# A fixed order of weights and additions on VectorE in the gather passes of a graph network

## Chip, core and metric

The kernel runs on one core of one Trainium2 chip. The metric is device time in microseconds (us) of one execution; less is better. PE is TensorE's matmuls and PEld its weight loads, DVE is VectorE, ACT is ScalarE, POOL is GpSimd, SP is SyncE. "L720" is line 720 of the kernel before the change.

## What is computed

Two layers, each a graph convolution followed by a feed-forward part, work on 6250 nodes with 256 float32 features and 100000 edges that are sorted by target node. The change touches the two sums over edges in the graph convolution of the second layer, which the code calls layer 1. Cut to what matters, the reference does this:

```python
def _hconv(x, src, dst, ew, w1, b1, w2, b2, g, b):
    h = relu(x @ w1 + b1)
    msg = ew[:, None] * h[src]                             # one row for each edge
    agg = segment_sum(msg, dst, num_segments=x.shape[0])   # sum by target node
    h = agg @ w2 + b2
    return relu(_bn(h, g, b))

residual = x
h = _hconv(x, src, dst, ew, c1_w1, ...)      # first pass
h = relu(_bn(h, bn1_g, bn1_b))
h = _hconv(h, src, dst, ew, c2_w1, ...)      # second pass
h = _bn(h, bn2_g, bn2_b)
out = relu(h + residual)
```

## The kernel before

Nodes are handled in 49 tiles of 128. The node values `h` of a convolution are in SBUF (`X`) and also in a table in DRAM. The sums by target node are in SBUF (`sums`, a view of the buffer `wide`, which is the name that the profile shows), as 49 blocks of 128 nodes.

The edges are cut into work items of 128 edges that all end in one block of targets. There are 830 items. Since the edges are sorted and the low targets are frequent, the first 407 items belong to the first 13 blocks. These 13 blocks are not gathered edge by edge: their edge weights have been written earlier into a dense matrix in DRAM (`S`), and a block's sum is a product of that matrix with the node tiles. The other 423 items are gathered. Both happen beside each other, in one loop, `gather_pass`, which runs once for each convolution: the first pass and the second pass.

For each gathered item k the loop issues:

- the **gather** (L720): POOL starts an indirect DMA that fetches the 128 source rows of `h` from the table into a buffer `g`. There are ten such buffers, so gather k can start when product k-10 is done.
- the **weights** (L591, in `chosen`): DVE writes a 128x128 matrix `sw` that has each edge's weight in the column of its target. Ten buffers.
- the **product** (L725): PE multiplies `sw` with `g` into a PSUM buffer `pm`. There are six, so product k can start when addition k-6 is done. In float32 a product shows as two weight loads and two matmuls in the profile.
- the **addition** (L727): DVE adds `pm` to the block of `sums` that the item belongs to. The block's number is read from a table on the chip: every 32 items one read loads 32 of these numbers for DVE (`block_of`).

Between the items the generator `dense_parts` puts the dense products: 13 blocks times 49 node tiles are 637 products (L1280) of a tile of `S` with a tile of `X`, accumulated over 49 into one of two PSUM buffers `dps`; after 49 DVE adds the block to `sums` (L1282). The tiles of `S` come by DMA through SP (L1274), seven tiles in a load of 448 KB, into the buffer `wide_b`, which holds two blocks. The loop asks for dense products so that they keep in proportion to the items:

```python
while done * (NK - k0) < (k - k0) * DB * NT:
    done += 1
    next(beside, None)
```

The text of the loop does not settle the order on an engine. A scheduler reorders the recorded instructions when the program is built, within their dependencies and the buffers; each engine then runs its own list strictly in order and waits by semaphores for the others. Only where the code says `keep_in_program_order` do instructions keep the place that the text gives them. In the passes of the kernel before nothing says so.

If the edges do not fit the dense form, another branch gathers all 830 items. It is in the program but is not taken here.

Of the kernel before, what the change touches and what calls it, by code (L numbers as in the profile page):

```python
# [7 lines left out]
F32 = mybir.dt.float32  # L8
I32 = mybir.dt.int32
AF = mybir.ActivationFunctionType  # L10
OP = mybir.AluOpType
# [3 lines left out]
P = 128  # L15
# [18 lines left out]
KG = (NK + P - 1) // P  # L34
NB = NT - 1
EG = 8
X0 = 8
H0 = 1024
X1 = 4
# [24 lines left out]
SQ = ST // P  # L64
NST = (2 * N + X0 * (ST - 1)) // ST
RW = D + X0
BNC = 250
# [9 lines left out]
    ("L1_gnn_bn2_g", 2), ("L1_gnn_bn2_b", 2),  # L77
    ("L0_ffn_ln_g", 2 * X0), ("L0_ffn_ln_b", 2 * X0), ("L0_ffn_b1", 8 * X0),
    ("L1_ffn_sb1", 2), ("L1_ffn_sb2", 1), ("L1_ffn_eb1", X1),
# [12 lines left out]
def gnn_ffn_kernel(ctx: ExitStack, tc: tile.TileContext, a: dict, out: bass.AP):  # L92
    nc = tc.nc
# [79 lines left out]
    lane = const.tile([P, P], F32, name="lane")  # L173
# [13 lines left out]
    def weight(pool, name, shape, src, **kw):  # L187
        t = pool.tile(shape, F32, name=name, **kw)
        nc.sync.dma_start(t, src)
        return t  # L190
# [188 lines left out]
    dl = const.tile([P, KG * P], F32, name="dl")  # L379
    w_e = const.tile([P, KG * P], F32, name="w_e")  # L380
# [198 lines left out]
    def block_of(k, engine, k0=0):  # L579

        if k % 32 == 0 or k == k0:
            g, j = k // P, k % P // 32 * 32
            blocks[:] = nc.values_load_multi_w_load_instructions(
                bk_i[g:g + 1, j:j + 32], engines=[engine], min_val=0, max_val=NT - 1,
                skip_runtime_bounds_check_because="counts at most as many blocks")[1]
        return blocks[k % 32]

    def chosen(k, wp):

        sw = wp.tile([P, P], F32, name="sw")  # L590
        nc.vector.tensor_scalar(sw, lane, dl[:, k:k + 1], w_e[:, k:k + 1], op0=OP.is_equal, op1=OP.mult)  # L591
        return sw

    def product_of_cells(nodes, lp, tp, pp):

# [50 lines left out]
    def scatter_items(k0, k1, nodes, pools, step):  # L646

        ep, wp, ptp, pmp = pools

        def equals(k0, k1):  # L650

            n = k1 - k0
            eq = ep.tile([P, EG, P], F32, name="eq")
            ct = ep.tile([P, EG], F32, name="ct")
            for q0 in range(0, n, 4):
                q1 = min(q0 + 4, n)
                pt = ptp.tile([P, 4, P], F32, name="pt")
                for i in range(q0, q1):
                    nc.tensor.transpose(pt[:, i - q0, :], s_f[:, k0 + i:k0 + i + 1].to_broadcast([P, P]), ident)
                for i in range(q0, q1):  # L660
                    nc.vector.scalar_tensor_tensor(eq[:, i, :], pt[:, i - q0, :], s_f[:, k0 + i:k0 + i + 1],
                                                   upto2[:, P:], op0=OP.is_equal, op1=OP.mult,
                                                   accum_out=ct[:, i:i + 1])
            off = ep.tile([P, EG], F32, name="off")
            idx = ep.tile([P, EG], I32, name="idx")
            sf = s_f[:, k0:k1]
            nc.vector.tensor_scalar(ct[:, :n], ct[:, :n], 1.5, None, op0=OP.is_gt)
            nc.vector.tensor_scalar(off[:, :n], sf, spare, -1.0, op0=OP.subtract, op1=OP.mult)
            nc.vector.tensor_tensor(off[:, :n], off[:, :n], ct[:, :n], OP.mult)
            nc.vector.tensor_tensor(idx[:, :n], off[:, :n], sf, OP.add)  # L670
            return eq, idx

        groups = {}
        pcs = pmp.tile([P, 4, P], F32, name="pcs", bufs=1)

        def group(k):
            g0 = k0 + (k - k0) // EG * EG
            if g0 < k1 and g0 not in groups:
                groups[g0] = equals(g0, min(g0 + EG, k1))
            return groups.get(g0), k - g0  # L680

        def begin(k):
            (eq, _), i = group(k)
            sw = chosen(k, wp)
            pc = pcs[:, k % 4, :]
            nc.tensor.matmul(pc, sw, eq[:, i, :], start=True, stop=True)  # L686
            cT = wp.tile([P, P], F32, name="cT")
            nc.scalar.copy(cT, pc)
            return cT

        begun = [begin(k) for k in range(k0, min(k0 + 2, k1))]
        for k in range(k0, k1):
            step(k)
            cT = begun.pop(0)
            if (k - k0) % EG == 2:
                group(k + EG)
            if k + 2 < k1:
                begun.append(begin(k + 2))
            bv = block_of(k, mybir.EngineType.PE, k0)
            pm = pmp.tile([P, D], F32, name="pm")  # L700
            nc.tensor.matmul(pm, cT, nodes[:, bass.ds(bv, 1), :].rearrange("p o d -> p (o d)"), start=True, stop=True)  # L701
            m = wp.tile([P, D], F32, name="m", bufs=10)
            nc.scalar.copy(m, pm)
            (_, idx), i = group(k)
            nc.gpsimd.indirect_dma_start(  # L705
                out=accs[k % NACC], out_offset=bass.IndirectOffsetOnAxis(ap=idx[:, i:i + 1], axis=0),
                in_=m, in_offset=None, compute_op=OP.add)

    def gather_pass(table, sums, k0=0, parts=None):

        with tc.tile_pool(name="gg", bufs=10) as gp, tc.tile_pool(name="gw", bufs=10) as wp, \
                tc.tile_pool(name="gpm", bufs=6, space=PSUM) as pmp:
            beside = parts(pmp) if parts else iter(())
            done = 0
            for k in range(k0, NK):
                while done * (NK - k0) < (k - k0) * DB * NT:
                    done += 1
                    next(beside, None)
                g = gp.tile([P, D], F32, name="g")
                nc.gpsimd.indirect_dma_start(  # L720
                    out=g, out_offset=None, in_=table,
                    in_offset=bass.IndirectOffsetOnAxis(ap=s_i[:, k:k + 1], axis=0))
                sw = chosen(k, wp)
                pm = pmp.tile([P, 1, D], F32, name="pm")
                nc.tensor.matmul(pm[:, 0, :], sw, g, start=True, stop=True)  # L725
                at = sums[:, bass.ds(block_of(k, mybir.EngineType.DVE, k0), 1), :]
                nc.vector.tensor_tensor(at, at, pm, OP.add)  # L727
            for _ in beside:
                pass

# [213 lines left out]
    with tc.tile_pool(name="f0c", bufs=1) as fc:  # L944
        wr = weight(fc, "wr", [P, KD, X0], a["L0_ffn_Wr"].rearrange("(k p) e -> p k e", p=P))
        brs = fc.tile([P, X0], F32, name="brs")
        nc.sync.dma_start(brs, bass.AP(tensor=a["L0_ffn_br"].tensor, offset=a["L0_ffn_br"].offset, ap=[[0, P], [1, X0]]))
        NPAR = 2 * KD + H0 // P
# [3 lines left out]
        with tc.tile_pool(name="f0x", bufs=2) as xp, tc.tile_pool(name="f0s", bufs=1) as sp, \  # L952
# [149 lines left out]
            for t0 in range(0, NT, TG):  # L1102
                for j in range(2):
# [3 lines left out]
                    for t in range(t0, t0 + TG):  # L1107
                        at_q = xp.tile([P, NQ], F32, name="at_q", bufs=4)
                        nc.vector.tensor_scalar(at_q, lane[:, :NQ], high_f[:, j, t:t + 1], tok_f[:, t:t + 1],
                                                op0=OP.is_equal, op1=OP.mult)  # L1110
# [110 lines left out]
    with ExitStack() as gs:  # L1221
# [21 lines left out]
        sums = nodes  # L1243
# [19 lines left out]
        def graph_pass(table):  # L1263
            with tc.If(fit > 0) as cmp:
                gather_pass(table, sums, KF, dense_parts)
            with cmp.Else():
                gather_pass(table, sums)
# [236 lines left out]
```

## Time and profile before

| | |
|---|---|
| median of 3 runs | 4724.84 us (4722.76 to 4731.99) |
| profiled execution, its own time | 4707.7 us |
| its span, first to last instruction | 4705.9 us |
| mean granted clock of TensorE | 0.886 of full speed |
| busy share of the span | PE 79%, PEld 59%, DVE 41%, ACT 22%, POOL 47% |
| first pass | from 2851 to 3469 us of the span |
| second pass | from 3610 to 4237 us of the span |
| gathers L720 | 846, 952 ns each, 805.5 us busy |
| products L725 | 1692 matmuls, 536.3 us busy |
| dense products L1280 | 2548 matmuls, 726.7 us busy |
| weights L591 | 1269 (423 of them in an earlier stage), 359 ns each |
| additions L727 | 846, 416 ns each, idle 622.1 us before them |

How to read it: the profile is of one execution, whose time lies a little below the median. A group's row gives, behind the number of its instructions, their busy time in us, the mean of one in ns, and how long the engine stood idle just before them, with what ended most of that idle time ("<-PE dps L1280 382.0": 382.0 us ended by a dense product on PE). "issue" means that nothing the profile shows was waited for. The ends of matmuls are modelled. Idle time of an engine that does not set the pace costs nothing.

### The profile page before, as it was taken

How to read it: one execution, taken by the hardware profiler on the slowest of the kernel's cores; microseconds unless marked ns; L12 is line 12 of the kernel's file. 1: busy time of each engine (PE TensorE's matmuls, PEld its weight loads, DVE VectorE, ACT ScalarE, POOL GpSimd, SP SyncE). 2: the span in 40 equal slices, each digit the busy share in tenths (PEclk: the TensorE clock that was granted, in tenths of full speed). 3: DMA queues.
4: the chain of work that ended last, by engine and by line, in shares of the span. 5: the costliest groups of instructions: out<-in, count | busy, mean ns of one | idle time of the engine just before them, and what ended most of it. 6: DMA issues, size and time to landing. Idle time of an engine off the chain costs nothing. (4 is left out here: it accounts for less than half of the span.)

```text
span 4705.9 us, 52220 instructions
## 1 busy us (share of the span) xinstructions
PE 3695.4 (79%) x16041; PEld 2767.7 (59%) x16041; DVE 1920.3 (41%) x7365; ACT 1035.2 (22%) x2388; POOL 2207.9 (47%) x1914
## 2 busy tenths in 40 slices
PE   2046658787778577799999977888896888887999
PEld 1013436676667336688888866666655666663444
DVE  6134333333444467522212244444444444445443
ACT  2000103333334233122222231000014000006443
POOL 2766664877778400133333315666632666660000
PEclk8578778989999785799999989999997999988999
DMA  9432363766666743366666655555414555550000
GB/s 349 102 111 72 93 243 83 104 103 102 105 102 85 143 131 105 119 195 190 193 196 196 188 139 191 160 153 161 146 44 155 155 154 160 157 152 21 18 19 19
DMA packets 393990, 625.11 MB, mean 133 GB/s; under 512 B 58935, under 2 KB 293450, under 8 KB 393690
## 3 DMA queue, kind: packets, MB, share of 16 engines
q1 hardware_dynamic: 241860, 394.88, 25.7%
q0 software_dynamic: 144176, 197.85, 22.4%
q10 hardware_dynamic: 7654, 28.78, 1.7%
q8 instruction: 140, 2.29, 0.2%
q14 instruction: 160, 1.31, 0.1%
HBM read 456.84 MB, written 165.69 MB: 132 GB/s over the span
## 5 line engine op out<-in xcount | busy, mean ns | idle before, releaser
L720 POOL DMA_INDIRECT g<-table,s_i x846 | 805.5, 952 | 589.1 <-issue 174.3
L705 POOL DMA_INDIRECT acc<-m,idx x423 | 654.5, 1547 | 204.6 <-issue 74.4
L1280 PE MATMUL dps<-X,wide_b 128*128 128x256 f32 (+1 forms) x2548 | 726.7, 401 | 11.7 <-issue 11.6
L725 PE MATMUL pm<-g,sw 128*128 128x256 f32 x1692 | 536.3, 407 | 212.3 <-issue 125.3
L727 DVE TENSOR_TENSOR wide<-wide,pm 128x256 f32 x846 | 351.9, 416 | 622.1 <-PE dps L1280 382.0
L1280 PEld LDWEIGHTS dps<-X,wide_b 128*128 128x128 f32 (+1 forms) x2548 | 516.6, 203 | 97.6 <-issue 17.3
L563 POOL DMA_INDIRECT S<-hv,hc x395 | 427.5, 1082 | 275.7 <-issue 106.8
L725 PEld LDWEIGHTS pm<-g,sw 128*128 128x128 f32 x1692 | 320.0, 199 | 328.7 <-issue 209.3
L591 DVE TENSOR_SCALAR sw<-lane,dl,w_e 128x128 f32<-128x128 f32 x1269 | 440.3, 359 | 114.8 <-PE dps L1280 49.3
L604 PE MATMUL cps<-wide,st 128*128 128x256 f32 x1274 | 362.0, 416 | 57.7 <-DVE X L609 23.1
L1181 PE MATMUL ph<-xe,we 128*128 128x256 f32 x1792 | 398.4, 381 | 0.0
L1190 PE MATMUL py<-we,hT 128*128 128x256 f32 x1792 | 396.0, 379 | 0.0
L1181 PEld LDWEIGHTS ph<-xe,we 128*128 128x128 f32 x1792 | 341.9, 191 | 47.4 <-issue 0.5
L1195 POOL DMA_INDIRECT mixed<-yo,to_i x112 | 178.3, 1592 | 394.1 <-DMA mixed<-yo,to_i 213.4
L1190 PEld LDWEIGHTS py<-we,hT 128*128 128x128 f32 x1792 | 336.2, 190 | 43.4
L1183 ACT ACTIVATE hT<-ph,par 128x256 f32<-128x256 f32 x448 | 212.4, 474 | 571.1 <-PE ph L1181 560.5
L741 ACT COPY hT<-tp 128x512 f32<-128x512 f32 (+1 forms) x75 | 40.3, 577 | 1352.8 <-PE tp L740 1352.8
L604 PEld LDWEIGHTS cps<-wide,st 128*128 128x128 f32 x1274 | 259.4, 209 | 106.0 <-issue 30.0
L701 PE MATMUL pm<-wide,cT 128*128 x846 | 269.2, 405 | 27.7 <-issue 26.1
L686 PE MATMUL pcs<-eq,sw 128*128 128x128 f32 x846 | 182.8, 300 | 133.7 <-DVE sw L591 83.5
L686 PEld LDWEIGHTS pcs<-eq,sw 128*128 128x128 f32 x846 | 148.5, 202 | 177.6 <-issue 85.7
L533 PE MATMUL h_pa<-h_eq,h_wd 128*8 128x256 f32 (+1 forms) x790 | 206.6, 418 | 38.9 <-DVE h_eq L527 25.5
(342 smaller groups left out, 4489.9 us busy)
## 6 DMA issues: line engine op xcount, KB each, us to landing
we<-in_L_ffn_W_dram SPq DMA_DIRECT2D x112, 1024.0 KB
wide_b<-S SPq DMA_DIRECT2D x182, 448.0 KB
S<-zz SPq DMA_DIRECT2D x13, 3136.0 KB
sb<-S SPq DMA_DIRECT2D x91, 448.0 KB
h_kb<-keys ACTq DMA_DIRECT2D x40, 576.0 KB
acc<-zero SPq DMA_DIRECT2D x3, 6400.0 KB
s<-acc SPq DMA_DIRECT2D x72, 256.0 KB
g<-table,s_i POOLq DMA_INDIRECT x846
```

The costliest lines, as they stand in the source:

```text
L563: sc = nc.gpsimd.indirect_dma_start(out=S.rearrange("(e o) -> e o", o=1), in_=hv[:, c:c + 1], in_offset=None, compute_op=OP.add if c < CA ...
L591: nc.vector.tensor_scalar(sw, lane, dl[:, k:k + 1], w_e[:, k:k + 1], op0=OP.is_equal, op1=OP.mult)
L604: nc.tensor.matmul(ps[:, j, :], st[:, i + j, :], nodes[:, b, :], start=(y == 0), stop=(y == len(sts) - 1))
L686: nc.tensor.matmul(pc, sw, eq[:, i, :], start=True, stop=True)
L701: nc.tensor.matmul(pm, cT, nodes[:, bass.ds(bv, 1), :].rearrange("p o d -> p (o d)"), start=True, stop=True)
L705: nc.gpsimd.indirect_dma_start(out=accs[k % NACC], out_offset=bass.IndirectOffsetOnAxis(ap=idx[:, i:i + 1], axis=0), in_=m, in_offset=None ...
L720: nc.gpsimd.indirect_dma_start(out=g, out_offset=None, in_=table, in_offset=bass.IndirectOffsetOnAxis(ap=s_i[:, k:k + 1], axis=0))
L725: nc.tensor.matmul(pm[:, 0, :], sw, g, start=True, stop=True)
L727: nc.vector.tensor_tensor(at, at, pm, OP.add)
L1181: nc.tensor.matmul(ps, we1[:, k, m * P:(m + 1) * P], xe[:, k, :], start=(k == 0), stop=(k == KD - 1))
L1190: nc.tensor.matmul(ps, hT[:, m, q * P:(q + 1) * P], we2[:, m, :], start=(m == 0), stop=(m == MH - 1))
L1280: nc.tensor.matmul(ps, sb[:r, t, :], X[:r, t, :], start=(t == 0), stop=(t == NT - 1))
```

## The change

In both passes the order of DVE's weights and additions is now given by the text of the loop. The additions are held in a list, `due`. When five items are in it (`LEAD = 5`), the oldest is added, and only then the weights of the current item are written; both are marked with `keep_in_program_order`. So DVE's list is: weights of the first five items, then in turn the addition of item k-5 and the weights of item k, and the last five additions at the end. `chosen` no longer makes its own tile and returns the instruction; the other place that calls it makes the tile itself, and is the same otherwise. Gathers, products and dense products are not marked; the scheduler places them as before, but sees another order on DVE.

```diff
+LEAD = 5
...
-    def chosen(k, wp):
-
-        sw = wp.tile([P, P], F32, name="sw")
-        nc.vector.tensor_scalar(sw, lane, dl[:, k:k + 1], w_e[:, k:k + 1], op0=OP.is_equal, op1=OP.mult)
-        return sw
+    def chosen(k, sw):
+
+        return nc.vector.tensor_scalar(sw, lane, dl[:, k:k + 1], w_e[:, k:k + 1], op0=OP.is_equal, op1=OP.mult)
...
             done = 0
+            due = []
+
+            def add_oldest():
+                k, pm = due.pop(0)
+                at = sums[:, bass.ds(block_of(k, mybir.EngineType.DVE, k0), 1), :]
+                tc.keep_in_program_order(nc.vector.tensor_tensor(at, at, pm, OP.add))
+
             for k in range(k0, NK):
...
-                sw = chosen(k, wp)
+
+                if len(due) == LEAD:
+                    add_oldest()
+                sw = wp.tile([P, P], F32, name="sw")
+                tc.keep_in_program_order(chosen(k, sw))
                 pm = pmp.tile([P, 1, D], F32, name="pm")
                 nc.tensor.matmul(pm[:, 0, :], sw, g, start=True, stop=True)
-                at = sums[:, bass.ds(block_of(k, mybir.EngineType.DVE, k0), 1), :]
-                nc.vector.tensor_tensor(at, at, pm, OP.add)
+                due.append((k, pm))
+            while due:
+                add_oldest()
             for _ in beside:
                 pass
```

More of the change, by code (lines that the diff above doesn't have):

```diff
@@ L683, in begin @@
             (eq, _), i = group(k)
-            sw = chosen(k, wp)
+            sw = wp.tile([P, P], F32, name="sw")
+            chosen(k, sw)
             pc = pcs[:, k % 4, :]
@@ L722, in gather_pass @@
                     in_offset=bass.IndirectOffsetOnAxis(ap=s_i[:, k:k + 1], axis=0))
-                sw = chosen(k, wp)
+                if len(due) == LEAD:
+                    add_oldest()
+                sw = wp.tile([P, P], F32, name="sw")
+                tc.keep_in_program_order(chosen(k, sw))
                 pm = pmp.tile([P, 1, D], F32, name="pm")
                 nc.tensor.matmul(pm[:, 0, :], sw, g, start=True, stop=True)
-                at = sums[:, bass.ds(block_of(k, mybir.EngineType.DVE, k0), 1), :]
-                nc.vector.tensor_tensor(at, at, pm, OP.add)
+                due.append((k, pm))
+            while due:
+                add_oldest()
             for _ in beside:
```

## The prediction

> **What bounds the kernel now.** I read the page first (where the chain runs in the passes of layer 1), then a table by stage, then groups and waits inside one pass, then the timeline, instruction by instruction. The code changes in two stretches only, the two passes, so everything else of the 4705.9 us span stays. By stage (us, then busy time and count of PE, PEld, DVE, ACT, POOL; granted clock; DMA share; GB/s):
>
> ```profile
> 2851.00:3469.00 618.00, 513.94 (x2105) 413.71 (x2106) 270.38 (x854) 0.00 (x0) 402.70 (x423) 0.94 0.51 156
> 3610.00:4237.00 627.00, 521.43 (x2120) 420.06 (x2120) 271.65 (x858) 0.00 (x0) 402.73 (x423) 0.93 0.53 163
> ```
>
> No engine fills a pass: PE is busy 83%, POOL 65%, DVE 43%. The groups of the second pass say what POOL and DVE wait for:
>
> ```profile
> L720 POOL DMA_INDIRECT g<-table,s_i x423 | 402.8, 952 | 286.7 <-issue 88.8 <-PE dps L1280 75.4 <-DMA wide_b<-S 73.9
> ...
> L727 DVE TENSOR_TENSOR wide<-wide,pm 128x256 f32 x423 | 175.8, 416 | 313.9 <-PE dps L1280 181.9 <-PE pm L725 82.8 <-remote 37.4
> ```
>
> POOL and DVE both wait for PE. How, the timeline of POOL shows (start, duration, idle before in brackets):
>
> ```profile
> 4052.68 0.95 POOL L720 DMA_INDIRECT g<-table,s_i  x1 [0.31 <-PE dps L1280]
> 4055.55 0.94 POOL L720 DMA_INDIRECT g<-table,s_i  x1 [1.93 <-PE dps L1280]
> 4056.80 0.95 POOL L720 DMA_INDIRECT g<-table,s_i  x1 [0.30 <-issue]
> ...
> 4064.39 0.94 POOL L720 DMA_INDIRECT g<-table,s_i  x1 [0.30 <-PE pm L725]
> 4066.45 0.95 POOL L720 DMA_INDIRECT g<-table,s_i  x1 [1.11 <-PE dps L1280]
> 4068.63 0.95 POOL L720 DMA_INDIRECT g<-table,s_i  x1 [1.23 <-PE dps L1280]
> ```
>
> A gather costs POOL 0.95 + 0.30 = 1.255 us. After about eight of them it stands still for 1.6 us more (1.93 less the usual 0.3; or two stops of 0.8 and 0.9). This repeats through the pass: 8 x 1.255 + 1.6 = 11.64 us for 8 items, 1.455 us an item; from the first gather (3609.92) to the last (4224.58) 422 steps take 614.7 us, 1.457 each. So POOL sets the pace, and its stops are the part that can change: 614.7 - 422 x 1.255 = 85 us a pass. Counted in the timeline by place: 9 us over the first 40 items, 42 over items 40 to 254, 33 over the last 165.
>
> Gather k needs the buffer of item k-10, that is, product k-10 done. What happens at a stop:
>
> ```profile
> 4046.40 0.59 PE L725 MATMUL pm<-g,sw 128*128 128x256 f32 x2
> ...
> 4053.45 1.03 PE L1280 MATMUL dps<-X,wide_b 128*128 128x256 f32 x4
> 4055.32 0.42 DVE L727 TENSOR_TENSOR wide<-wide,pm 128x256 f32 x1 [2.19 <-PE dps L1280]
> 4055.48 4.67 SPq L1274 DMA_DIRECT2D wide_b<-S  x2
> 4055.55 0.94 POOL L720 DMA_INDIRECT g<-table,s_i  x1 [1.93 <-PE dps L1280]
> 4055.79 0.70 PE L725 MATMUL pm<-g,sw 128*128 128x256 f32 x2 [1.31 <-issue]
> ```
>
> The first line is product 295, counted along the program's order. It is over at 4047.0; its addition starts at 4055.32, 8.3 us later, in the same instant as POOL and SP go on. So in these passes a product's completion reaches the others late (the median over the pass is 5.4 us), and what is held back comes at once when POOL stops. PE has meanwhile run to item 300 and stopped as well: product 301 starts 0.05 us after the end of addition 295, since the products have six PSUM buffers. One stop of POOL therefore frees six items (295 to 300); with what trickles through while POOL runs (2 items in 8 gathers), that gives the eight.
>
> **The change part by part.** *VectorE's order.* Before, the scheduler lets the weights run ahead: from item 40 on the weights of item k stand behind the addition of item k-10 or k-11, so they are long there and a product waits on DVE only for the addition six places back. After, weights k stand directly behind addition k-5 in both passes. Same instructions, 423 additions (0.416 us) and 422 to 423 weights (0.35 us) a pass, nothing added. But product k now waits for weights k, so for addition k-5, so for product k-5 to have been seen: PE runs five items past the last one seen, not six. Behind the weights nothing else is queued but the next addition; DVE's 43% cover their 0.34 us.
> The price goes by POOL's stops. A stop frees five items instead of six; with the same trickle in proportion (six make eight), 5 x 8/6 = 6.67 gathers from stop to stop. The last 165 items, where PE's order remains as it is, have 33 us of stops; 33 x 8/6.67 = 39.5, so +6.5 us a pass. PE keeps up: 6.67 items x 1.23 us busy (521/423) are 8.2 of the 10 us that a cycle lasts.
>
> *PE's order.* No instruction of PE changes, but the scheduler lays them anew. Before, the 637 dense products stand evenly among the 423 items from item 36 on, with seven or eight in a row every 18 items. After, between items 31 and 230 there are rows of 31, 34, 39, 20, 31 (11 and 20, two items apart), 32 and 18, and between them 25 to 30 items with one dense product to two items. While such a row runs, POOL can go on only until its ten buffers are full. The nearest row of before is one of 17, behind item 9:
>
> ```profile
> 3629.75 6.21 PE L1280 MATMUL dps<-X,wide_b 128*128 128x256 f32 x28
> ...
> 3639.47 0.59 PE L725 MATMUL pm<-g,sw 128*128 128x256 f32 x2
> ```
>
> It holds PE for 9.7 us, and POOL loses 3.1 us in it (idle 0.87, 0.84 and 2.34 us, less 0.31 each). So POOL's cover is 9.7 - 3.1 = 6.6 us. A dense product takes 6.21/28 x 2 = 0.444 us with its tail, 0.432 without; over the mean clock of 0.93 that is 0.465. The seven rows take 14.4, 15.8, 18.1, 9.3, 14.4, 14.9 and 8.4 us; less 6.6 each, POOL loses 7.8 + 9.2 + 11.5 + 2.7 + 7.8 + 8.3 + 1.8 = 49 us. A row also clears all that is held back; after the row of 17 the next stop came twelve gathers later, where eight is usual. I therefore leave one stop of 1.6 us to each of the seven stretches between rows: 11 us. Sum 60 against 42, +18 us a pass. With the next stops at twelve and at nineteen gathers, as after the row of 17, it is +29; with the full ten buffers as cover (12.55 us), 26 against 42, -16.
>
> *Start.* Before, dense rows of 10 and 17 and short leads of 1 to 4; after, even at first. The first 40 items took 1.43 and 1.48 us each in the two passes, close to the rest. I take 0, with 9 us of stops as the bound of a gain.
> *SP's and POOL's queues.* Same order. Each load of wide_b waits for dense products two blocks back (98 of them), so a row of 39 has its data in place: 0.
>
> Sum: 2 x (6.5 + 18) = +49 us. The profiled execution took 4707.7 us (span 4705.9, 1.8 around it), 17 below the median of 4724.84; I put the difference on the median: **4774 us**.
>
> A rule against the row: the Trainium skill, *TensorE: Matmul & The Clock Gate*, section "The cost: per-tile semaphore tail", has completions that follow each other cost some 26 ns apiece. By it the round of product, addition, weights would be under 2 us in five items' 7.3 us, and the new order would cost nothing; the median of 5.4 us above decides against it here.
>
> **The rivals.**
> *Faster (0.15).* The rows of dense products are the mechanism: they clear what is held back and, if POOL has its full ten buffers at their start, cost less than the stops that they replace: -16 + 6.5 = -9.5 us a pass, 4706 us. For it: POOL alone would need only 530 us a pass. Against it: cover in the row of 17 was 6.6 us. It decides from a cover of about 10.7 us: the seven rows then cost 24 us, with 11 of stops 35, 7 less than 42, which pays the 6.5 us.
> *No change (0.11).* Completions are seen in time for five items and the cover lies between: 4725 us. Outside the passes products are picked up in time (in the expert layer ACT's L1183 starts 0.04 us after its product, by the median); against it stands that PE's stops of before all end at addition k-6, the very limit that shrinks.
> *Much slower (0.12).* PE becomes the pace. It has 77 gaps in the second pass, 92 us in sum. If each new wait lasts until the next addition and its weights are done (0.585 us from addition to addition, + 0.34 of weights = 0.9 us more), that is 77 x 0.9 = 69 us a pass, +138, 4863 us. Against it: PE has 2 us to spare in each cycle of POOL's.
>
> **How the numbers follow.** My case has 0.62 (4734 to 4835). 0.2%, 9.4 us, is about what a measurement here can tell from no change. Faster 0.15, within 0.11, slower 0.74. The range leaves out half of the faster case and about all of the much slower one: 4718 to 4838.
>
> **What would show it.** Right: POOL's stops in the last 165 items come every six to seven gathers, still 1.6 us; long stops of 8 to 11 us at the rows of 31 to 39; each product behind a PE gap starts just after its weights (L591), not after L727; passes of about 640 and 650 us. Wrong: the same eight between stops (then five or six is not the limit), rows that cost POOL under 3 us, or a change outside 2851 to 3469 and 3610 to 4237.

## The result and the profile after

The changed kernel takes 4798.82 us (median of 4 runs, 4792.69 to 4808.21) against 4723.80 us (4 runs, 4719.11 to 4731.99) in the same comparison: a ratio of 1.0158, 95% interval 1.0133 to 1.0184. It is 75 us slower; 4774 us with a range of 4718 to 4838 was predicted. The profiled execution took 4796.46 us, its span 4794.7, 88.8 more than before. In the changed code the gather is L727, the addition L720, the product L736, the dense product L1292, the weights still L591.

By stage, the two passes (us, then busy time and count of PE, PEld, DVE, ACT, POOL; granted clock; DMA share; GB/s):

```profile
2838.00:3502.00 664.00, 527.47 (x2107) 422.00 (x2108) 267.69 (x847) 0.00 (x0) 400.59 (x423) 0.91 0.47 145
3642.00:4310.00 668.00, 530.24 (x2109) 427.29 (x2110) 268.56 (x848) 0.00 (x0) 400.61 (x423) 0.89 0.49 151
```

The instructions in them are the same, and PE's busy time is only 13.5 and 8.8 us more, at a lower granted clock (0.91 and 0.89 instead of 0.94 and 0.93). From the first gather to the last a pass takes 661.0 and 664.1 us, where it took 614.0 and 614.7: 96.4 us more in the two together. The rest of the span is 7.6 us shorter, in code that the change doesn't touch (the first pass already begins 13.7 us earlier). The groups of the second pass:

```profile
L727 POOL DMA_INDIRECT g<-table,s_i x423 | 400.6, 947 | 337.5 <-PE pm L736 96.4 <-issue 75.9 <-DMA wide_b<-S 73.1
...
L720 DVE TENSOR_TENSOR wide<-wide,pm 128x256 f32 x418 | 174.8, 418 | 339.3 <-PE pm L736 139.0 <-PE dps L1292 98.5 <-remote 86.4
```

A gather costs POOL what it cost, 0.947 us. Its idle time has grown from 286.7 to 337.5 us. Where, the timeline of POOL shows. At the row of 39 dense products:

```profile
3809.12 0.94 POOL L727 DMA_INDIRECT g<-table,s_i  x1 [0.30 <-issue]
3810.36 0.95 POOL L727 DMA_INDIRECT g<-table,s_i  x1 [0.30 <-PE dps L1292]
3825.01 0.94 POOL L727 DMA_INDIRECT g<-table,s_i  x1 [13.70 <-PE pm L736]
3826.26 0.94 POOL L727 DMA_INDIRECT g<-table,s_i  x1 [0.30 <-PE pm L736]
```

and the timeline of PE at the same place:

```profile
3803.78 1.19 PE L736 MATMUL pm<-g,sw 128*128 128x256 f32 x2 [2.35 <-remote]
3804.77 19.54 PE L1292 MATMUL dps<-X,wide_b 128*128 128x256 f32 x78
3824.14 0.59 PE L736 MATMUL pm<-g,sw 128*128 128x256 f32 x2
```

78 matmuls are 39 dense products in one piece of 19.54 us. The product that POOL's next buffer needs comes only behind them, and POOL goes on 0.3 us after its end: 13.70 us of idle time, 13.4 more than the usual 0.30 (10.6 more at the same gather of the first pass). In the last 165 items, where PE's order is the old one, the small stops go on:

```profile
4104.55 0.94 POOL L727 DMA_INDIRECT g<-table,s_i  x1 [1.94 <-PE dps L1292]
4105.79 0.94 POOL L727 DMA_INDIRECT g<-table,s_i  x1 [0.30 <-issue]
...
4113.47 0.94 POOL L727 DMA_INDIRECT g<-table,s_i  x1 [0.48 <-PE pm L736]
4116.39 0.94 POOL L727 DMA_INDIRECT g<-table,s_i  x1 [1.98 <-PE dps L1292]
```

All stops of POOL beyond the usual 0.305 us, summed over the gathers of the timeline by place (us, first and second pass):

| items | before | predicted after | after |
|---|---|---|---|
| 0 to 39 | 6.9, 8.7 | the same | 7.0, 8.0 |
| 40 to 254 | 42.2, 42.3 | 60 | 88.0, 89.4 |
| of it while one of the seven rows runs | – | 49 | 60.2, 58.0 |
| of it between the rows | – | 11 | 27.8, 31.4 |
| last 165 | 34.5, 33.2 | 39.5 | 37.2, 38.4 |

By place the stops grow by 48.6 and 51.7 us a pass; the gather itself, 0.947 us instead of 0.952, takes some 2 us of that back.

### The profile page after: what moved, and what is told of

Same layout as the page of the kernel before. It is cut to its first block, busy times and chain, and to the rows that moved or that the text cites. A ratio compares the mean times of both kernels' runs of the same rounds, so it can differ in the third digit from the quotient of the medians.

```text
span 4794.7 us, 52236 instructions
## 1 busy us (share of the span) xinstructions
PE 3727.7 (78%) x16041; PEld 2790.1 (58%) x16041; DVE 1920.0 (40%) x7365; ACT 1034.9 (22%) x2388; POOL 2204.1 (46%) x1914
## 4 chain that ended last, share of the span: by engine, by line
PE 64%; issue 10%; DMA 8%; another core or an unknown queue 8%; DVE 7%; POOL 2%; ACT 2%; DVEq 0%; SPq 0%; ACTq 0%; POOLq 0%
PE dps L1292 13%; PE pm L736 9%; PE ph L1193 8%; PE py L1202 8%; PE cps L603 4%; DMA acc<-m,idx 3%; PE dense L271 3%; PE h_pa L534 2%; DMA S<-hv,hc 2%; PE hid L1248 2%; PE ph L1443 2%; PE pm L701 2%; PE py L1468 1%; POOL S L564 1%
## 5 line engine op out<-in xcount | busy, mean ns | idle before, releaser
L727 POOL DMA_INDIRECT g<-table,s_i x846 | 801.8, 948 | 688.8 <-PE pm L736 189.6
L736 PE MATMUL pm<-g,sw 128*128 128x256 f32 x1692 | 550.2, 426 | 284.2 <-remote 105.7
L1292 PE MATMUL dps<-X,wide_b 128*128 128x256 f32 (+1 forms) x2548 | 700.5, 400 | 6.5 <-issue 6.5
L720 DVE TENSOR_TENSOR wide<-wide,pm 128x256 f32 x846 | 354.1, 419 | 674.6 <-PE pm L736 288.4
L736 PEld LDWEIGHTS pm<-g,sw 128*128 128x128 f32 x1692 | 335.5, 210 | 410.6 <-remote 152.0
L1292 PEld LDWEIGHTS dps<-X,wide_b 128*128 128x128 f32 (+1 forms) x2548 | 518.1, 203 | 90.1 <-issue 8.9
L591 DVE TENSOR_SCALAR sw<-lane,dl,w_e 128x128 f32<-128x128 f32 x1269 | 439.0, 358 | 21.1 <-PE pcs L686 19.7
```

The lines of the kernel that those rows point to most:

```text
L591: return nc.vector.tensor_scalar(sw, lane, dl[:, k:k + 1], w_e[:, k:k + 1], op0=OP.is_equal, op1=OP.mult)
L720: tc.keep_in_program_order(nc.vector.tensor_tensor(at, at, pm, OP.add))
L727: nc.gpsimd.indirect_dma_start(out=g, out_offset=None, in_=table, in_offset=bass.IndirectOffsetOnAxis(ap=s_i[:, k:k + 1], axis=0))
L1292: nc.tensor.matmul(ps, sb[:r, t, :], X[:r, t, :], start=(t == 0), stop=(t == NT - 1))
```

## Experiments

They ran on two other chips, on which the kernel before takes 4412 to 4417 us instead of 4724; so each is compared only with the kernel before that ran beside it, and the two kernels of the case were run there too. (The record names these two chips, but not the one of the recorded runs; that it is a third one, and not one of the two in another condition, is inferred from the times.)

**Both kernels again.** The kernel before, once:

> The kernel before once more, for its profile on this set's chip. If completions are late (median 5.4 us), POOL's stops are 84 us a pass; if they are prompt, POOL's stops are under 5 us a pass and a pass takes some 535 us instead of 622.

It took 4403.08 us (span 4401.3). The changed kernel, against 4411.72 us of the kernel before beside it:

> The kernel after the change once more, beside the experiments of this set. In the set before this one the chip showed additions that start 0.04 us after their product (median) and no stops of POOL with even order, unlike the profiles of before and after. Theory 'rows': on a chip with prompt completions the ratio is 1.013 as with the rows alone (rows cost 27 us a pass); on one with late completions 1.016 as measured, with 45 to 50 us a pass more stops than before. If the ratio is under 1.005 on a prompt chip, rows and a lead of five together are not what rows alone are.

It took 4464.28 us, ratio 1.0124 (1.0087 to 1.0161), so 53 us slower there instead of 75. The groups of the second pass of the kernel before on this chip, and a product with its addition from the timeline:

```profile
L720 POOL DMA_INDIRECT g<-table,s_i x423 | 400.9, 948 | 206.1 <-DMA wide_b<-S 74.6 <-PE pm L725 46.4 <-PE dps L1280 45.4
...
L727 DVE TENSOR_TENSOR wide<-wide,pm 128x256 f32 x423 | 177.2, 419 | 231.2 <-PE pm L725 216.7 <-PE dps L1280 7.2 <-issue 5.9
```

```profile
3799.91 0.59 PE L725 MATMUL pm<-g,sw 128*128 128x256 f32 x2
...
3800.54 0.42 DVE L727 TENSOR_TENSOR wide<-wide,pm 128x256 f32 x1 [0.18 <-PE pm L725]
```

The product ends at 3800.50, its addition starts 0.04 us later, and 0.04 us is the median of both passes; in the recorded profile of before it was 5.5 and 5.4 us. POOL's stops are 1.8 and 2.8 us a pass instead of 84, and a pass takes 531 us from the first gather to the last, close to 422 x 1.255. The small stops of the prediction's eight-item cycle are thus absent on these chips, and what is left of the change shows alone: 29.0 and 30.5 us a pass, all but 2 at five gathers (numbers 42, 75, 107, 173 and 205, those that wait for the first product behind a row), among them 7.3 and 8.0 us at number 107. The timelines of PE and POOL in the changed kernel on this chip, at the row of 39 in the second pass:

```profile
3558.09 17.00 PE L1292 MATMUL dps<-X,wide_b 128*128 128x256 f32 x78
```

```profile
3566.57 0.95 POOL L727 DMA_INDIRECT g<-table,s_i  x1 [0.31 <-PE dps L1292]
3575.80 0.94 POOL L727 DMA_INDIRECT g<-table,s_i  x1 [8.28 <-PE pm L736]
```

**VectorE's new order alone.** The changed kernel with TensorE's two matmuls pinned as well, so that PE keeps the loop's even mix and no rows form:

```diff
-                nc.tensor.matmul(pm[:, 0, :], sw, g, start=True, stop=True)
+                tc.keep_in_program_order(nc.tensor.matmul(pm[:, 0, :], sw, g, start=True, stop=True))
...
-                    nc.tensor.matmul(ps, sb[:r, t, :], X[:r, t, :], start=(t == 0), stop=(t == NT - 1))
+                    tc.keep_in_program_order(nc.tensor.matmul(ps, sb[:r, t, :], X[:r, t, :], start=(t == 0), stop=(t == NT - 1)))
```

> VectorE's order as after the change (weights five places behind), but PE's order is fixed as the text has it: one or two dense products in front of each item, no rows. Theory 'rows' (most of the loss is POOL standing still while PE runs a row of 18 to 39 dense products, and the stops between the rows): the long stops vanish, POOL's stops fall from about 134 us a pass to about 90, time 4730 to 4745 us. The prediction's other term (a stop frees five items, not six): stops every 6.7 gathers, +17 us a pass, 4758 us. Rival 'lead' (the weights that stand later make the loss, the rows are harmless): about 4799 us.

4416.92 us against 4416.58, ratio 0.9999 (0.9980 to 1.0017); stops of 1.3 and 2.1 us a pass. POOL's group in the second pass has 205.4 us of idle time, where the kernel before has 206.1 on the other of the two chips:

```profile
L727 POOL DMA_INDIRECT g<-table,s_i x423 | 400.9, 948 | 205.4 <-DMA wide_b<-S 74.6 <-PE dps L1292 44.8 <-PE pm L736 43.3
```

Run a second time beside the changed kernel:

> As the first run of this edit (weights five behind, PE's order even). Theory 'rows': within 0.5% of before on either kind of chip; with late completions the last 165 items may cost 4 to 6 us more a pass, as after shows there, so ratio 1.000 to 1.004. The prediction's term of five instead of six: 1.007 on a chip with late completions. Rival 'lead': 1.013 or more where completions are late.

1.0003 (0.9983 to 1.0023). So weights behind the addition five places ahead cost nothing that can be measured on these chips. What they cost where completions are late, the two runs cannot say.

**TensorE's even order alone.** The same two pins in the kernel before:

> The kernel before, with PE's order fixed as the text has it and VectorE left to the scheduler (weights ten places ahead). Both theories: as before, 4724 us within 10, since before had nearly this order; POOL's stops 80 to 86 us a pass. More than that would mean that pinning PE costs by itself, and e1 has to be read against this run.

4412.43 us, ratio 0.9986 (0.9970 to 1.0002): the pins on PE are not what costs either, and gain nothing that can be told from zero.

**The rows alone.** The kernel before with PE pinned to the order that the scheduler made in the changed kernel, while the weights stay ten places ahead (the list of 423 counts of dense products is cut here; the dense product is pinned as in the run before):

```diff
+ROWS = [ord(c) - 97 if c >= "a" else ord(c) - 39 for c in (
...
-                while done * (NK - k0) < (k - k0) * DB * NT:
+                while parts and done < sum(ROWS[:k - k0 + 1]):
...
-                nc.tensor.matmul(pm[:, 0, :], sw, g, start=True, stop=True)
+                tc.keep_in_program_order(nc.tensor.matmul(pm[:, 0, :], sw, g, start=True, stop=True))
...
```

> PE's order is fixed to that of the kernel after, rows of 11 to 39 dense products at the same items, and VectorE is left to the scheduler (weights ten places ahead). Theory 'rows': long stops of 7 to 13 us at the rows as after, POOL's stops 120 to 135 us a pass, 4785 to 4800 us. Rival 'lead': 4724 to 4735 us.

4469.85 us against 4416.58, ratio 1.0130 (1.0094 to 1.0165), as much as the whole change (1.0124). The stops are 28.0 and 28.8 us a pass, at the same five gathers. POOL's timeline at the row of 39:

```profile
2866.46 0.94 POOL L726 DMA_INDIRECT g<-table,s_i  x1 [0.30 <-PE dps L1286]
2875.09 0.94 POOL L726 DMA_INDIRECT g<-table,s_i  x1 [7.69 <-PE pm L731]
```

In the traces the 2120 matmuls of a pass stand in the same order here as in the changed kernel; in the first experiment it is VectorE's additions and weights that stand in the changed kernel's order, and PE's are even. So on these chips the loss goes with the rows, and an effect of VectorE's own order, if there is one, is below the 0.2% of the interval.

**Is it the five places?** The changed kernel with ten, about where the kernel before has most weights; the rows come out as 36, 39, 39, 20, 33, 37 and 20:

```diff
-LEAD = 5
+LEAD = 10
```

> The changed kernel with ten places instead of five, about where the kernel before has the weights of most items; the pins on VectorE stay and TensorE is left to the scheduler, which now forms rows of 36, 39, 39, 20, 33, 37 and 20 dense products. Theory (the loss comes from the rows, which the scheduler forms because VectorE's order is pinned, whatever the number of places): stops of about 6.9, 7.5, 7.5, 0 to 1, 6, 7 and 0 to 1 us = 35 us a pass instead of 29, and a ratio of 1.013 to 1.018. Rival (the loss comes from the five places): with ten the stops go, and the ratio is 0.998 to 1.003.

4485.09 us against 4417.12, ratio 1.0152 (1.0134 to 1.0171), stops of 37.6 and 39.3 us a pass. More room did not help: the rows are longer and the stops with them. (The two ratios, 1.0152 and 1.0124, have intervals that overlap.) With five and with ten places the scheduler forms rows; no run has the additions' new place in the text without the pins, so which of the two makes it do so is not shown.

**How near may the weights come?** PE even as in the first experiment, and two places:

```diff
-LEAD = 5
+LEAD = 2
```

> The weights come behind the addition of the item two places ahead, instead of five; TensorE's two matmuls are pinned in the order in which they are written, one or two dense products behind each product. Theory (the later place costs only when the loop product, addition, weights, product is longer than its items' share of POOL's pace): 0.40 + 0.42 + 0.36 = 1.2 us and some tenths for three semaphores, with up to 0.8 us behind dense products 2.0 to 2.3 us, against 2 x 1.255 = 2.5 us: no stop of POOL, ratio 0.998 to 1.003. Rival (each place nearer costs by itself, the wait of the weights on the addition): 423 x 2 times some tenths, a ratio of 1.02 or more.

4416.70 us, ratio 1.0001 (0.9983 to 1.0018), stops of 1.2 and 2.1 us a pass. So even at two places the wait of the weights on the addition costs nothing here, as the theory had it; a shorter distance, where it would begin to cost, was not run.

**More cover.** The changed kernel with sixteen gather buffers:

```diff
-        with tc.tile_pool(name="gg", bufs=10) as gp, tc.tile_pool(name="gw", bufs=10) as wp, \
+        with tc.tile_pool(name="gg", bufs=16) as gp, tc.tile_pool(name="gw", bufs=10) as wp, \
```

> The changed kernel with sixteen buffers for the gathered rows instead of ten; the order of every engine, the rows of dense products included, stays. Theory (TensorE's rows hold POOL because ten buffers are the only cover): the runs with rows showed stops of 2.9 to 8.0 us at five gathers of a pass; six more buffers are six more gathers of 1.255 us, 7.5 us of cover, so all of them go but for some tenths, a pass's gathers take 531 us instead of 559, and the ratio is 0.998 to 1.002. Rival (what costs is the addition of five places ahead on VectorE, or TensorE itself losing the time): the stops move or stay, and the ratio stays at 1.010 to 1.014.

4416.61 us against 4417.12, ratio 1.0002 (0.9988 to 1.0017). The row of 39 in the second pass in PE's timeline, POOL's timeline behind it, and POOL's group in that pass:

```profile
3531.07 17.31 PE L1292 MATMUL dps<-X,wide_b 128*128 128x256 f32 x78
```

```profile
3546.12 0.95 POOL L727 DMA_INDIRECT g<-table,s_i  x1 [0.30 <-PE dps L1292]
3549.09 0.95 POOL L727 DMA_INDIRECT g<-table,s_i  x1 [2.02 <-PE pm L736]
```

```profile
L727 POOL DMA_INDIRECT g<-table,s_i x423 | 401.6, 949 | 207.0 <-DMA wide_b<-S 74.6 <-PE dps L1292 47.5 <-PE pm L736 47.1
```

207.0 us idle, against 206.1 in the kernel before there. The rows are as long as ever, and one stop is left of them in the two passes: 1.7 us beyond the usual 0.3 at gather 113, which waits for the product behind this row. Sixteen buffers cover 15.4 of its 17.1 us, and all of every other row.

**Less cover.** Seven buffers, which makes it about as thin as it was in the recorded profile:

```diff
-        with tc.tile_pool(name="gg", bufs=10) as gp, tc.tile_pool(name="gw", bufs=10) as wp, \
+        with tc.tile_pool(name="gg", bufs=7) as gp, tc.tile_pool(name="gw", bufs=10) as wp, \
```

> The changed kernel with seven buffers for the gathered rows instead of ten, so that the cover at a row of dense products is about what it was in the recorded profile (there 6.6 us were reckoned; here ten buffers cover some 10 us, and three fewer take 3 x 1.255 = 3.8 us of it). Theory A (the 35 us a pass of small stops between the rows come with late completions, not with a thin cover): stops at the seven rows alone, about 8.9, 10.1, 11.1, 2.5, 6.7, 9.2 and 2 us = 50 us a pass, under 5 us between them, and a ratio of 1.021 to 1.026. Theory B (a cover used up by a row is not regained before the next, so POOL goes on stopping between them): 15 us a pass or more between the rows, and a ratio over 1.030.

4523.72 us, ratio 1.0234 (1.0210 to 1.0258). PE and POOL at the row of 39:

```profile
3609.10 17.00 PE L1292 MATMUL dps<-X,wide_b 128*128 128x256 f32 x78
```

```profile
3614.45 0.95 POOL L727 DMA_INDIRECT g<-table,s_i  x1 [0.30 <-PE dps L1292]
3626.81 0.94 POOL L727 DMA_INDIRECT g<-table,s_i  x1 [11.41 <-PE pm L736]
```

In the first pass the seven rows stop POOL for 8.4, 10.1, 11.1, 4.4, 6.5, 9.2 and 2.7 us, 52.4 in sum, and everything else for 2.4 us; in the second it is 50.4 and 3.7. Most of the rows' part of the recorded loss (60.2 and 58.0) is reproduced; the small stops between the rows (27.8 and 31.4) are not. A thin cover alone does not make them.

**POOL's pace.** The kernel before without POOL's gathers: ACT issues a plain load of 128 rows of the table instead, so the sums are not over the sources.

```diff
-                nc.gpsimd.indirect_dma_start(
-                    out=g, out_offset=None, in_=table,
-                    in_offset=bass.IndirectOffsetOnAxis(ap=s_i[:, k:k + 1], axis=0))
+                nc.scalar.dma_start(g, table[(k % 48) * P:(k % 48 + 1) * P])
```

> The kernel before, but each item's 128 rows come by a contiguous load of the table on ScalarE's queue instead of a gather by POOL (so the sums over edges are of other rows). If product completions are held back by POOL's gathers: additions start within 0.2 us of their product by the median instead of 5.4, PE gaps at the additions vanish, a pass takes 500 to 540 us, some 180 us less in all. If the lateness is PE's own or comes of the waits between PE and VectorE: the median lateness stays at 4 to 6 us and a pass over 580 us.

4268.95 us (once more, 4265.66 us). From the first addition to the last a pass takes 464 us, 1.10 an item, where the kernel before beside it takes 527 and 531. So POOL does set the pace, and the other engines have about 65 us a pass to spare behind it. Additions start 0.04 us after their product (median) in both runs, as they do with the gathers on these chips; so whether POOL's gathers hold completions back on the recorded chip stays open.

> As the first run of this edit (contiguous loads on ScalarE's queue in place of POOL's gathers; the sums are of other rows). On a chip with late completions it tells whether POOL's gathers hold them back: then additions start within 0.2 us of their product; otherwise the median lateness stays at 4 to 6 us. On a chip with prompt completions: as before, some 148 us less than the kernel before, since POOL no longer sets the pace.

The second run is 146 us below the kernel before beside it (148 were expected). Of the runs that compute the same sums, none beats the kernel before by more than can be measured.

## Why the prediction was right, and by which steps

The sign and the place held: the loss lies in the two passes, POOL sets their pace, and its stops grow. These steps stand.

*The rows.* They cost what their length is beyond the cover of the ten buffers, and the lengths were right: for the six that stand alone 14.4, 15.8, 18.1, 9.3, 14.9 and 8.4 us were reckoned, 81 in sum, and the timeline of the second pass has 13.5, 14.7, 19.4, 9.9, 13.8 and 7.8, 79 in sum. That the buffers are the cover is shown by changing their number on the other chips. The row of 34 in the second pass, from its first dense product to the next product, had the same length in all four runs:

| run | buffers | row of 34, us | POOL's stop, us | cover, us | cover at each of the six, second pass, us |
|---|---|---|---|---|---|
| changed, recorded | 10 | 14.7 | 9.1 | 5.6 | 4.0 to 5.6 |
| changed, other chip | 10 | 14.7 | 6.4 | 8.3 | 8.1 to 8.9, all of the rows of 20 and 18 |
| changed, other chip | 7 | 14.7 | 9.9 | 4.8 | 4.7 to 5.8 |
| changed, other chip | 16 | 14.7 | 0 | all | 15.4 of the row of 39, all of the others |

Three buffers less are 3.5 us less at this row (3.8 were expected). In the second pass on the recorded chip ten buffers cover no more than seven do on the other. The row took 14.7 us there in a pass with a mean granted clock of 0.89, and the same 14.7 us on the other chip in a pass with 0.97; so the lower clock did not lengthen it. The rival "faster" needed a cover of about 10.7 us; the rows of that pass that stopped POOL had at most 5.6 us on the recorded chip and 8.9 on the other. That the change works, on the other chips, through the order of a neighbour and not through the wait that it adds is the rows' run beside the even run: 1.0130 and 0.9999.

*What ends PE's gaps.* Before, 123 of 143 gaps over 0.3 us ahead of a product ended within 0.12 us of an addition's end; after, 125 of 134 end within 0.12 us of the end of weights, and none so near to an addition. (The prediction had all of PE's stops of before end at an addition; it was most.) In the timeline of DVE and PE:

```profile
4104.31 0.42 DVE L720 TENSOR_TENSOR wide<-wide,pm 128x256 f32 x1 [2.20 <-PE dps L1292]
...
4104.65 0.34 DVE L591 TENSOR_SCALAR sw<-lane,dl,w_e 128x128 f32<-128x128 f32 x1
4104.90 0.41 DVE L720 TENSOR_TENSOR wide<-wide,pm 128x256 f32 x1
4105.09 0.67 PE L736 MATMUL pm<-g,sw 128*128 128x256 f32 x2 [1.34 <-PE dps L1292]
```

The weights end at 4104.99, and the product starts 0.10 us later.

*The small terms.* Start 0 (measured +0.1 and -0.7 us), queues of SP and POOL 0 (the idle time that loads of `wide_b` end for POOL is 73.1 us in the second pass, 73.9 before).

*PE as the pace.* Against the much slower rival: on the other chip, with the same rows and the same wait, sixteen buffers bring the time back to that of the kernel before (1.0002), and without POOL's gathers a pass is some 65 us shorter. On the recorded chip PE is busy 530 of the 668 us of the second pass, as it was 521 of 627.

Three terms of the sum were off. By place the sum of the two passes should have been 49 us and is 100; as the gathers and the rest of the execution were a little quicker, the span grew by 88.8 and the median by 75.

*"So POOL's cover is 9.7 - 3.1 = 6.6 us."* At the rows of the recorded run it was 4.0 to 5.6 us in the second pass. In the first, the rows of 34 and 39 also took longer than reckoned, 17.8 and 22.5 us, with pauses of PE of 2.2 and 3.4 us in them. The rows cost 60.2 and 58.0 us instead of 49: 11 and 9 us a pass too little. One row of before was taken for all, and in the second pass each of the six had less cover than it.

*"I therefore leave one stop of 1.6 us to each of the seven stretches between rows: 11 us."* Measured: 27.8 and 31.4 us, so 17 and 20 us a pass too little; 37 us of the span, the largest miss. In the second pass the first stop comes ten or eleven gathers behind that of a row (53 behind 42, 85 behind 75, 117 behind 107), but others follow it before the next row, 4.0 and 4.5 us a stretch instead of 1.6. The one stop behind the row of 17 was too little to go by. The run with seven buffers excludes a thin cover as the sole cause: there the rows stop POOL nearly as long, with hardly a stop between them. It leaves the late completions of the recorded runs, which none of the experiments had; that they are the cause is argued, not shown.

*"A stop frees five items instead of six; with the same trickle in proportion (six make eight), 5 x 8/6 = 6.67 gathers from stop to stop."* The five are there: behind the stop of the fence above, DVE adds five items in a burst, from 4104.31 to 4106.66. But the stops still come every eight to nine gathers, which the prediction named as a sign of being wrong ("the same eight between stops (then five or six is not the limit)"): three more items trickle through before the next burst, where two were taken. The median lateness has fallen from 5.5 and 5.4 us to 3.8 and 3.3, and a quarter of the additions now start within 1.2 us of their product. The last 165 items lose 2.7 and 5.2 us a pass by stops that are a little longer, where 6.5 was reckoned from their number: the form was wrong, and that the second pass comes near in size is luck. That five instead of six is what makes them longer is argued, not shown: where completions are prompt, neither five places nor two cost anything.

The Trainium skill, *TensorE: Matmul & The Clock Gate*, section "The cost: per-tile semaphore tail", was weighed against the row of 5.4 us. On the two other chips the same interval, from a product's end to its addition, is 0.04 us by the median, and there the new order on VectorE costs nothing, as the estimate from that page's 26 ns for one more completion had it; on the recorded chip it is 5.4 us, and no run here says what delayed it. So what the wait itself costs on the recorded chip was not separated from the rest; the rows cost on all of the chips, 60.2 and 58.0 us a pass on the recorded one and 27 to 28 on the others. Why completions come late on one chip and not on others stays open, and so does what sixteen buffers or a pinned TensorE would give on that chip: none of the experiments ran there.

## What to carry to other kernels

Where a scheduler lays out the engines, pinning one engine's order moves the others too: compare the instruction order of every engine before and after, and price what has moved on the engine that feeds the pacing one. A long piece of other work on a producer costs its length less the cover that the consumer's buffers give; measure that cover at more than one such piece already in the trace (here 6.6 us at one, and 4.0 to 5.6 at six of the rows that came), and pin the producer as well or add buffers, both of which took the loss away on the other chips. A periodic stop whose cause is not known should not be assumed away by a single quiet stretch behind one event.

## What was not expected of the hardware

The kernel before has a span of 4705.9 us on the recorded chip and 4401.3 on another. 166 of these 305 us are in the two passes (614.0 and 614.7 us of gathers against 530.8 and 531.5), while a gather costs POOL the same on both, 952 and 948 ns. The granted clock of the passes is 0.94 and 0.93 on the recorded chip, 0.99 on the other, which is a few per cent; a product's end reaches VectorE after a median of 5.4 us on the one and 0.04 us on the other.
